# Cross-attention on one core: the right sums of the last batch's product 4 ahead of block 12, and twelve warming matmuls

## The chip, the cores and the metric

The kernel runs on one core of a Trainium2 chip. The metric is the device time of one execution in microseconds. A core has a matrix engine (TensorE, PE in the profile, with its weight loads as PEld), three engines for elementwise work (VectorE or DVE, ScalarE or ACT, GpSimd or POOL), and a queue engine that only issues transfers (SyncE or SP). The engines run their own instruction lists in order, and wait for each other through semaphores. TensorE writes into banks of an accumulator memory (PSUM), from which VectorE and ScalarE read.

## The reference

There are 8 batches of a 512 x 1024 input x1 and a context x2 of the same shape, all in f32.

```python
B, C1, C2, N = (8, 512, 512, 1024)      # D = C2 // 8 = 64
q = einsum('bcn,dc->bnd', x1, Wq) + bq
k = einsum('bcn,dc->bdn', x2, Wk) + bk[:, None]
v = einsum('bcn,dc->bdn', x2, Wv) + bv[:, None]
attn = softmax(einsum('bnd,bdm->bnm', q, k), axis=2)
out = einsum('bcm,bnm->bcn', v, attn) + x1
```

## The kernel before

Each batch goes through one call of `period`. The kernel reorders the algebra: instead of projecting values first, it multiplies the context with the exponentials of the scores (`first`, stage "y") and then the result with the value weights (`second`, stage "o"). Both are products of two 2 x 2 block matrices, done in seven block products in place of eight. These need sums and differences of blocks on the left (S1 to S4) and on the right (T1 to T4), which VectorE forms, and sums of the seven results, which VectorE forms when it empties the banks. The table `MULT` gives for each product its left and right operand, its pair of banks ("a" or "c"), and whether it opens them. In the branch that the change touches, stage "y" has the order 1, 2, 6, 5, 7, 3, 4.

Some block products are done with the same seven-fold scheme once more inside (`multiply_2`, `multiply_7`, `multiply_3`, `multiply_4`): then `inner_left` (L355) and `inner_right` (L367) form the inner sums on VectorE, `inner_product` (L374) multiplies on TensorE, two matmuls of 256 columns for each of the seven small products, and ScalarE copies some of the results out (L383). For product 4 the small products come in the order 1, 7, 6, 2, 5, 4, 3. Small product 1 takes the blocks as they are, 7 takes the third right sum, 6 the second, 5 the first and 4 the fourth. Small products 1, 6 and 5 add up in one shared bank, and ScalarE copies it after each; 7 and 4 use another, copied after 7 into a buffer v.

`multiply_3` does the matmuls of product 3 and returns a function, here called `evict_3`. When that is called, VectorE first adds v to the second half of the copies d (`complete`, L452) and then adds d to the two "a" banks to give block 12 of the y matrix (L483). Products 3 and 4 use the same buffer for v.

The right operand of product 4, called T4, is made in `sum_t4`: in the later batches ScalarE copies one block (L278), and two transfers issued by GpSimd add another on top (L280).

After products 3 and 4, `evict_y` empties the other blocks (L502) and multiplies all by the reciprocal softmax sums (L507, L505), `sum_y` forms the right sums T1 to T4 of the outer stage (L262), and `second` multiplies with the value weights in the order 1, 6, 2, 5, 7, and in the last batch 4 and 3. `evict_o` adds bias and x1 and sends the result (L526 to L539).

All of it is in an order written out by hand (`manual_schedule`): what stands first in the text is first on its engine. In batches 2 to 5 and in the last, batch 7, the branch `seven` of `period` is taken; `n` is the following batch, and None in the last one. Batches with a following one have its scores and exponentials mixed in as hooks.

The kernel begins with `head`: it issues loads of the weights, x1 and x2, clears a 128 x 128 tile named `warm` on VectorE, multiplies it with itself `WARM` times on TensorE (L635), and then projects the first batch's queries (L586) and keys (L601) as the tiles arrive. Scores (L191), the running maximum (L659, L668), the maximum over partitions on GpSimd (L221), the subtraction (L243) and the exponentials (L244) follow, up to the first large product at L321.

Of the kernel before, what the change touches and what calls it, by code (L numbers as in the profile page):

```python
# [15 lines left out]
def kernel(  # L16
# [51 lines left out]
    CT = C // P  # L68
    H = 512
    MH = N // P // 2  # L70
    WARM = 10
    lo, hi = slice(0, D), slice(D, 2 * D)

    const = ctx.enter_context(tc.tile_pool(name="const", bufs=1))
# [171 lines left out]
    def lower(s, h, i):  # L246
        e = s.e[h][:, :, i, :]
        top = s.top[h].unsqueeze(1).to_broadcast([P, 2, H])
        nc.vector.tensor_tensor(e, e, top, ALU.subtract)  # L249

    def exponential(s, h, i):
        e = s.e[h][:, :, i, :]
        nc.scalar.activation(e, e, AF.Exp)  # L253

    def exponentials(s, h, i):
        lower(s, h, i)
        exponential(s, h, i)
# [91 lines left out]
    def inner_left(s, i, x, tag):  # L349

        v = {f"{p + 1}{q + 1}": x[:, ts(q, MH // 2), ts(p, P)] for p in range(2) for q in range(2)}
        sums = sb.tile([P, 4, MH // 2, P], F32, tag=tag, name=f"aI{i}_{s.b}")
        for z, (k, x, y, op) in enumerate(LEFT):
            v[k] = sums[:, z]
            nc.vector.tensor_tensor(v[k], v[x], v[y], op)  # L355
        s.inner[i] = v

    def inner_right(s, i, x, *tags):

        v = {  # L360
            f"{q + 1}{r + 1}": x[:, ts(q, MH // 2), ts(r, H // 2)] for q in range(2) for r in range(2)
        }
        shape = [P, 4 // len(tags), MH // 2, H // 2]
        sums = [sb.tile(shape, F32, tag=t, name=f"eI{i}{t}_{s.b}") for t in tags]
        for z, (k, x, y, op) in enumerate(RIGHT):
            v[k] = sums[z // shape[1]][:, z % shape[1]]
            nc.vector.tensor_tensor(v[k], v[x], v[y], op)  # L367
        s.inner[i, "t"] = v
# [95 lines left out]
    def multiply_7(s, hooks):  # L464

        d, complete = multiply_onto(s, 7, "i2", "y12", hooks)

        def add():
            complete()
            for k in (5, 6):  # L470
                nc.vector.tensor_tensor(s.tmp[k], s.tmp[k], d, ALU.add)

        return add

    def multiply_3(s, hooks):

        d, complete = multiply_onto(s, 3, "u1", "r", hooks)

        def evict():
            complete()  # L480
            s.y["12"] = y = sb.tile([P, 2, H], F32, tag="y12", name=f"y12_{s.b}")
            for j in (1, 0):
                nc.vector.tensor_tensor(y[:, j, :], s.bank["a", j], d[:, j, :], ALU.add)  # L483

        return evict
# [4 lines left out]
    def evict_y(s, k, steps=(1, 2)):  # L490

        bank, add = RESULT[k]
        rden = s.rden.get(int(k[1]) - 1)
        if 1 in steps:
            s.y[k] = sb.tile([P, 2, H], F32, tag=f"y{k}", name=f"y{k}_{s.b}")
        y = s.y[k]
        alone = 7 in s.inner and add in (5, 6)
        for step in steps:
            for j in range(2):
                if step == 1:  # L500
                    ps, n = s.bank[bank, j], left if alone and j else slice(0, H)
                    nc.vector.tensor_tensor(y[:, j, n], ps[:, n], s.tmp[add][:, j, n], ALU.add)  # L502
                elif alone and j:
                    for x, n in ((y, left), (s.tmp[add], right)):
                        nc.vector.tensor_tensor(y[:, j, n], x[:, j, n], rden[:, n], ALU.mult)  # L505
                else:
                    nc.vector.tensor_tensor(y[:, j, :], y[:, j, :], rden, ALU.mult)  # L507
# [49 lines left out]
    def copy_first(s, h):  # L557

        s.mx[h] = sb.tile([P, 2, H], F32, tag="fold", name=f"sum_{s.b}_{h}", bufs=2)
        nc.scalar.copy(s.mx[h], s.e[h][:, :, 0, :])  # L560

    def start_sum(s, h):

        copy_first(s, h)
        for i in range(1, MH if s.b > 1 else 2):
            add_tile(s, h, i)
# [40 lines left out]
    def head(s):  # L609
# [23 lines left out]
        ps = ps_a.tile([P, H], F32, tag="a0", name="ps_warm")  # L633
        for _ in range(WARM):
            nc.tensor.matmul(ps[:, 0:P], warm, warm, start=True, stop=True)  # L635
# [72 lines left out]
    def period(s, n, nn, nnn):  # L708
# [5 lines left out]
        def first(i, hook=None):  # L714
            multiply(s, "y", i, s.a, s.t, MH, hook=hook)
# [47 lines left out]
        def add_exponential(i):  # L763
            exponential(n, 0, i)
            add_tile(n, 0, i)
# [20 lines left out]
        if seven:  # L786
            hooks = [{}, {}]
            if n:
                for i in range(MH):
                    lower(n, 0, i)  # L790
                hooks = [
                    {
                        1: lambda: copy_first(n, 0),
                        6: lambda: add_exponential(1),
                        5: lambda: add_exponential(2),
                    },
                    {6: lambda: add_exponential(3)},
                ]
            first(5, (lambda: exponential(n, 0, 0)) if n else None)
            inner_right(s, 3, s.t["22"], "eT1")  # L800
            inner_left(s, 4, s.a["22"], "a12")
            add_7 = multiply_7(s, hooks[0])
            add_7()
            evict_3 = multiply_3(s, hooks[1])
            evict_y(s, "22", (1,))
            evict_3()
            inner_right(s, 4, s.t["T4"], "eT2")
        else:
            first(5)
            if s.b == 0:  # L810
                inner_right(s, 3, s.t["22"], "eT1")
                for i in range(MH):
                    lower(n, 0, i)
            else:
                for i in range(MH):
                    exponentials(n, 0, i)
                start_sum(n, 0)
                inner_right(s, 3, s.t["22"], "eT1")
            first(7)
            if s.b > 1:  # L820
                inner_right(s, 4, s.t["T4"], "eT2")
            evict_3 = multiply_3(s, {})
            if s.b:
                evict_y(s, "22", (1,))
                evict_3()
            else:
                evict_3()
                evict_y(s, "22", (1,))
# [70 lines left out]
    with tc.manual_schedule():  # L899
        head(states[0])  # L900
        for b in range(B):
            period(*states[b : b + 4])
# [31 lines left out]
```

## Time and profile before

| | us |
|---|---|
| median of 3 runs | 693.46 (693.18 to 695.86) |
| the profiled execution | 693.62 |
| its span, first to last instruction | 691.8 |
| TensorE busy | 682.8 |
| VectorE busy | 628.9 |
| ScalarE busy | 276.1 |
| GpSimd busy | 193.5 |

A busy time is the sum of the times in which an engine had at least one instruction at work. A large f32 matmul of 128 x 512 appears as two rows, and so does each warming matmul. Rows of TensorE overlap: a new row begins before the last one has ended, so the pace is read from the starts. In a line of the timeline the first number is the start in microseconds from the beginning of the span, the second the duration, and "x8" the number of rows merged into it; brackets give the idle time of the engine just before and what ended it.

### The profile page before, as it was taken

What the parts mean: (1) busy time and instruction counts of PE and PEld (TensorE: products, weight loads), DVE (VectorE), ACT (ScalarE), POOL (GpSimd) and SP (SyncE); (2) the same over time, 40 slices, a digit from 0 to 9 for tenths busy, and PEclk for the clock granted to TensorE, in tenths of its full rate; (3) what the DMA queues carried; (4) which work ended last, traced back from release to release, by engine and by line L of the source; (5) the groups of instructions that cost most, each with busy time, mean ns of one, the idle gap of its engine ahead of it and who ended that gap; (6) DMA issues with size and microseconds to landing.
All of it is one profiled execution on the core that took longest, in us unless ns stands there. A gap on an engine that the chain in (4) does not pass through costs nothing.

```text
span 691.8 us, 6647 instructions
## 1 busy us (share of the span) xinstructions
PE 682.8 (99%) x2248; PEld 364.2 (53%) x2248; DVE 628.9 (91%) x809; ACT 276.1 (40%) x439; POOL 193.5 (28%) x147
## 2 busy tenths in 40 slices
PE   9999999999999999999999999999999999999997
PEld 5333554535545565455644566454754545545753
DVE  1999999988999889998999989999799988999785
ACT  2733353146233552345432454424544245243220
POOL 0123113522423223242142321623223232323000
PEclk9999999999999999999999999999999999999999
DMA  9676256954569754786628867198642864268303
GB/s 304 258 214 238 65 182 130 255 161 79 183 114 235 199 106 153 150 231 181 135 111 180 230 181 187 42 198 215 167 92 38 207 166 76 62 148 223 87 0 122
DMA packets 44723, 109.05 MB, mean 158 GB/s; under 512 B 4880, under 2 KB 7184, under 8 KB 44688
## 3 DMA queue, kind: packets, MB, share of 16 engines
q1 hardware_dynamic: 25856, 70.13, 30.1%
q0 software_dynamic: 17424, 36.25, 29.7%
q10 hardware_dynamic: 1408, 2.23, 1.0%
q8 instruction: 18, 0.29, 0.2%
q14 instruction: 17, 0.14, 0.1%
HBM read 72.62 MB, written 16.81 MB: 129 GB/s over the span
## 4 chain that ended last, share of the span: by engine, by line
PE 93%; DMA 3%; DVE 1%; SPq 1%; ACT 1%; issue 0%; DVEq 0%
PE ps_ya L321 24%; PE ps_i L374 17%; PE ps_oa L321 16%; PE ps_oc L321 12%; PE ps_s L191 6%; PE ps_yc L374 5%; PE ps_q L149 4%; PE ps_k L149 3%; PE ps_yc L321 3%; PE ps_ya L374 3%; DMA a<-in_x2T_dram 1%; DMA x_in_x_dram<-in_x_dram 1%; DMA x_head<-in_x_dram 1%; PE ps_sc L191 1%; PE ps_sa L191 1%; DVE aS L110 0%
## 5 line engine op out<-in xcount | busy, mean ns | idle before, releaser
L321 PE MATMUL ps_ya<-eT,aS 128*128 128x512 f32 x256 | 113.1, 595 | 0.0
L332 ACT COPY uy<-ps_ya 128x512 f32<-128x512 f32 x48 | 28.1, 588 | 139.6 <-PE ps_ya L321 126.7
L249 DVE TENSOR_TENSOR e<-e,top 128x1024 f32<-128x1024 f32 x60 | 70.5, 1228 | 11.0 <-POOL top L221 11.0
L321 PEld LDWEIGHTS ps_ya<-eT,aS 128*128 128x128 f32 x256 | 48.0, 190 | 60.9 <-issue 58.5
L253 ACT ACTIVATE e<-e 128x1024 f32<-128x1024 f32 x60 | 62.9, 1059 | 38.6 <-DVE e L249 37.1
L221 POOL PARTITION_ALL_REDUCE top<-max x16 | 32.8, 2052 | 150.8 <-DVE max L215 78.9
L226 POOL PARTITION_ALL_REDUCE den<-sum x16 | 63.4, 3961 | 40.8 <-DVE sum L215 35.8
L321 PE MATMUL ps_oa<-yT,w_S 128*128 128x512 f32 x128 | 57.6, 593 | 0.0
L321 PE MATMUL ps_oc<-y,w 128*128 128x512 f32 x128 | 57.6, 593 | 0.0
L321 PE MATMUL ps_ya<-e,a 128*128 128x512 f32 x128 | 56.3, 593 | 0.3 <-ACT e L244 0.3
L200 ACT COPY e<-ps_s 128x1024 f32<-128x1024 f32 x46 | 45.7, 1027 | 19.3 <-PE ps_s L191 17.5
L332 ACT COPY uo<-ps_oa 128x512 f32<-128x512 f32 x48 | 27.6, 584 | 54.2 <-PE ps_oa L321 44.9
L383 ACT COPY d<-ps_i 128x256 f32<-128x256 f32 x84 | 29.3, 374 | 47.7 <-PE ps_i L374 47.2
L191 PE MATMUL ps_s<-q,k 64*128 64x512 f32 x188 | 47.3, 608 | 0.8 <-ACT q L590 0.8
L551 POOL DMA_DIRECT2D uo<-in_x_dram x21 | 24.9, 1186 | 79.2 <-DVE uo L548 79.2
L555 POOL DMA_DIRECT2D sum<-e x21 | 25.7, 1222 | 66.5 <-DMA sum<-e 37.0
L321 PEld LDWEIGHTS ps_ya<-e,a 128*128 128x128 f32 x128 | 24.2, 190 | 31.3 <-issue 29.6
L321 PEld LDWEIGHTS ps_oa<-yT,w_S 128*128 128x128 f32 x128 | 24.2, 190 | 30.8 <-issue 29.9
L321 PEld LDWEIGHTS ps_oc<-y,w 128*128 128x128 f32 x128 | 24.1, 190 | 31.0 <-issue 28.9
L211 DVE TENSOR_TENSOR max<-max,e 128x1024 f32<-128x1024 f32 x30 | 36.8, 1225 | 3.0
L507 DVE TENSOR_TENSOR y<-y,den 128x512 f32<-128x512 f32 x54 | 33.8, 683 | 0.0
L238 POOL DMA_DIRECT2D den<-row x16 | 8.9, 557 | 79.0 <-DMA row<-few 73.2
(142 smaller groups left out, 1291.4 us busy)
## 6 DMA issues: line engine op xcount, KB each, us to landing
x_in_x_dram<-in_x_dram SPq DMA_DIRECT2D x60, 512.0 KB, 5.9
a<-in_x2T_dram SPq DMA_DIRECT2D x32, 512.0 KB, 7.1
sum<-e POOLq DMA_DIRECT2D x21, 512.0 KB, 5.2
uo<-in_x_dram POOLq DMA_DIRECT2D x21, 512.0 KB, 6.5
out_dram<-uo SPq DMA_DIRECT2D x21, 512.0 KB, 5.1
eT<-eT POOLq DMA_DIRECT2D x12, 512.0 KB, 6.5
den<-row POOLq DMA_DIRECT2D x16, 256.0 KB, 3.6
r<-in_x_dram POOLq DMA_DIRECT2D x7, 512.0 KB, 8.6
```

What stands on the lines that cost most here:

```text
L149: nc.tensor.matmul(ps[r, :], w_sb[:, c, :], s.x[:, c, ts(h, H)], start=(c == 0), stop=(c == CT - 1),)
L191: nc.tensor.matmul(ps[g], s.k[r, ts(i, P)], s.q[r, ts(h, H)], start=True, stop=True)
L200: nc.scalar.copy(e[:, :, i, :], whole)
L211: nc.vector.tensor_tensor(f, e[:, :, 0, :] if i == 1 else f, e[:, :, i, :], op)
L221: nc.gpsimd.partition_all_reduce(s.top[h], s.mx[h][:, 0, :], P, ReduceOp.max)
L226: nc.gpsimd.partition_all_reduce(s.den[h], s.mx[h][:, 0, :], P, ReduceOp.add)
L249: nc.vector.tensor_tensor(e, e, top, ALU.subtract)
L253: nc.scalar.activation(e, e, AF.Exp)
L321: nc.tensor.matmul(ps[:, n], left[ka][:, k, ts(j, P)], right[kb][:, k, n], start=opens and k == 0, stop=i in (2, 3, 4) and k == n_k - 1, s ...
L332: nc.scalar.copy(s.tmp[i][:, j, :], ps)
L374: nc.tensor.matmul(ps, s.inner[i][ka][:, k, :], s.inner[i, "t"][kb][:, k, :], start=opens and k == 0, stop=z in (2, 3, 4) and k == MH // 2 ...
L507: nc.vector.tensor_tensor(y[:, j, :], y[:, j, :], rden, ALU.mult)
```

## The change

In the last batch (the one with no following batch) the four right sums of product 4 are formed on VectorE before block 12 is emptied; in the other batches of the branch the order stays. The number of warming matmuls goes from ten to twelve.

```diff
-    WARM = 10
+    WARM = 12
...
             evict_3 = multiply_3(s, hooks[1])
             evict_y(s, "22", (1,))
-            evict_3()
+            if n:
+                evict_3()
             inner_right(s, 4, s.t["T4"], "eT2")
+            if not n:
+                evict_3()
```

On VectorE this gives, in the last batch, the instructions L502, L502, four times L367, L452, L483, L483, where before it was L502, L502, L452, L483, L483, four times L367. The instruction lists of ScalarE, GpSimd and SyncE are the same as before, and TensorE's differs by the two matmuls.

## The prediction

> **What bounds the kernel now.** First the shares of busy time and the slices on the page. TensorE is busy for all but 9.0 of 691.8 us, in nearly every slice, at a granted clock of 1.00 in every stretch read. So a change pays only where TensorE stands still, and costs only where it makes TensorE later.
>
> ```profile
> span 691.8 us, 6647 instructions
> PE 682.8 (99%) x2248; PEld 364.2 (53%) x2248; DVE 628.9 (91%) x809; ACT 276.1 (40%) x439; POOL 193.5 (28%) x147
> ```
>
> Next, TensorE's own list of waits (engine, line, what it waited for: us in total, times, longest). One wait stands far above the rest, and it is in the last batch: product 4 waits for VectorE's right sums (L367).
>
> ```profile
> PE ps_i L374 <- DVE eI4eT L367: 2.3, 1, 2.3
> PE ps_warm L635 <- DVE warm L632: 1.0, 1, 1.0
> PE ps_s L191 <- ACT q L590: 0.8, 1, 0.8
> ```
>
> Then the timeline around that wait (start, duration, engine, line; idle time and releaser in brackets), VectorE first. Between 653.33 and 654.49 VectorE idles for the copies of product 3; then it adds d and v, evicts block 12 (L483), and only then forms the four sums.
>
> ```profile
> 652.31 1.01 DVE L502 TENSOR_TENSOR y<-ps_yc,uy 128x512 f32<-128x512 f32 x2
> 654.49 0.69 DVE L452 TENSOR_TENSOR d<-d,v 128x512 f32<-128x512 f32 x1 [1.16 <-ACT d L383]
> 655.29 1.29 DVE L483 TENSOR_TENSOR y<-ps_ya,d 128x512 f32<-128x512 f32 x2
> 656.49 0.68 DVE L367 TENSOR_TENSOR eI4eT<-eT 128x512 f32<-128x512 f32 x1
> 657.82 0.68 DVE L367 TENSOR_TENSOR eI4eT<-eT 128x512 f32<-128x512 f32 x1
> ...
> 658.65 1.97 PE L374 MATMUL ps_i<-eI4eT,aI 128*128 128x256 f32 x8 [2.28 <-DVE eI4eT L367]
> ```
>
> Product 4 runs its small products in the order 1, 7, 6, 2, 5, 4, 3. The first needs no sum (it started at 655.34); the second needs the third sum, T3. TensorE started 0.15 us after T3 ended (657.82 + 0.68 = 658.50).
>
> Last the start. The ten warming matmuls leave twenty rows, two for each f32 matmul, and the first projection then waits for its data.
>
> ```profile
> 1.04 4.62 PE L635 MATMUL ps_warm<-warm 128*128 128x128 f32 x20 [1.04 <-DVE warm L632]
> L635 PEld LDWEIGHTS ps_warm<-warm x20: 288/333/338, 1.0 to 5.1; 128*128 128x128 f32 x20
> 5.90 1.08 PE L586 MATMUL ps_q<-x_head,wqk_sb 128*64 128x512 f32 x4 [0.23 <-DMA x_head<-in_x_dram]
> 9.35 1.96 PE L601 MATMUL ps_kc<-x_head,wqk_sb 128*64 128x256 f32 x16
> 11.50 0.65 PE L601 MATMUL ps_ka<-x_head,wqk_sb 128*64 128x256 f32 x4 [0.19 <-DMA x_head<-in_x_dram]
> ```
>
> **Part 1: the sums ahead of block 12.** Nothing is added or removed, and no DMA, matmul or copy moves: on VectorE, in the last batch alone, four 128x512 sums change places with one add and two evictions.
>
> When can the sums start? The second L502 of the pair starts at 652.91 and holds 256 columns; the next instruction follows such a one after 0.34 us (L505 to L505, 662.03 to 662.37), so at 653.25. The sums also wait for T4, which two accumulating transfers finish. They are issued by 637.05, and the longest transfer into eT takes 10.6 us to land: 647.7, 5.5 us earlier. And T4's first small product ran at 655.34 with no wait. Inside the group the starts lie 0.71, 0.61 and 0.60 apart (656.49, 657.21, 657.82, 658.42), so T3 starts at 654.57 and ends at 655.25; with the 0.15 us of release TensorE could go at 655.40.
>
> When does TensorE want it? Small products follow each other every 0.86 us (652.75, 653.61, 654.47, 655.34), so at 656.20. The slack is 0.8 us, and the wait goes entirely. Its price is best taken by pace: product 3, the same work without a stall, takes 655.34 - 649.29 = 6.05 us; product 4 takes 663.90 - 655.34 = 8.56 us. Gain **2.51 us** (the 2.28 us of visible idling and the refilling of the pipeline).
>
> What is late next? The displaced instructions:
> - The add (L452) starts after the fourth sum, at 653.25 + 1.92 + 0.60 = 655.77, and ends at 656.47 instead of 655.18. ScalarE's copy of the next v uses the same buffer; it comes 1.06 us after the second small product begins (650.16 to 651.22 in product 3), so at 657.26. Slack 0.8 us. Queued behind it on ScalarE are the copies of small products 6 and 5, and TensorE's shared bank waits for those: past this slack, each lost microsecond returns to TensorE.
> - The evictions (L483) end at 657.87. The bank is wanted by the next stage at 655.34 + 6.05 = 661.39.
> - The VectorE chain after them no longer contains the idle 1.16 us, so it runs about 1.2 us earlier, while TensorE runs 2.51 us earlier: TensorE catches up by 1.3. Tightest is the outer product 6, which needs yT2. It ends now at 663.95 + 1.22 = 665.17, afterwards at 663.97, released by 664.1; TensorE wants it at 667.33 - 2.51 = 664.82. Slack 0.7 us. Block 21 is complete at 669.19 - 1.2 = 668.0; its first half, wanted at 668.26, is ready by 667.4.
> - From there VectorE waits for TensorE (1.23 us before the next L534), and the output transfers follow it. The whole tail moves.
>
> Value taken -2.51; bounds -2.51 and, if the VectorE chain did not move up at all, 665.17 + 0.15 - 664.82 = 0.5 less, -2.0.
>
> **Part 2: two more warming matmuls.** Four more rows. The nearest row is the warming itself: its row starts lie 0.2133 us apart after the first, up to 5.26. Four more at that pace push the next free slot from 5.47 to 6.33, and the projection from 5.90 to 6.33: +0.43 us. The sixteen key rows after it have almost no pause to absorb that (eight pairs at 0.2155 are 1.72 us, and 0.05 us is lost to the DMA wait inside), so +0.37 us reaches ScalarE's key copy, and along the chain key copy, scores, maximum, all-reduce, subtraction, exponential, everything up to the first large product at 24.96. VectorE goes through that stretch back to back, so nothing there takes it up. The exponential that waits for the last warming matmul (L645, 5.70) may slip by 0.86 us freely: ScalarE's next work is at 9.59.
>
> [...] The projection already runs at full pace from 5.90 (two rows per 0.43 us). [...] By the row, +0.37. [...]
>
> [...]
>
> **Sum.** -2.51 + 0.2 = -2.3 us. On the profiled execution: span 691.8 to 689.5, its time 693.62 to 691.3. The median of the runs, 693.46, stands 0.16 lower: **691.2 us**, -0.33%. What a measurement of this kernel can tell from no change is about 0.5% or 3.5 us, which is more than the entire wait.
>
> **Rivals.**
> - *The wait moves instead of going.* If the VectorE chain stays where it is, outer product 6 waits 0.5 us: 691.7. For: the margin is only 0.7 us. Against: 1.16 us of VectorE idling really is filled.
> - *It does not do what it says.* If the last arrival was T4's transfer and not T3, nothing is won: 693.46 + 0.2 = 693.7. Against: T4's raw block was multiplied at 655.34 without waiting.
> [...]
> - *Slower.* The head's delay makes the next batch's context load collide. That load is issued from 36.78 on, after the queries, and TensorE's keys wait for its last tile at 46.88. If a 2 MB block of another queue went ahead of it at the 404 GB/s of the head, 5.2 us: 691.2 + 5.2 = 696.4. It decides once the load lands 2.3 us later than now, the whole gain. For: TensorE waits there already. Against: a shift of 0.2 us moves issue and need alike.
>
> **How the numbers follow.** The forecast 0.80 (its own range 690.6 to 691.8: head 0 to +0.37, product 4 -2.51 to -2.3, and some tenths between runs), wait moved 0.07, no effect 0.04, faster 0.05, slower 0.04. The range of 690.2 to 692.8 takes in the moved wait and the scatter of the three runs (a median may lie some tenths off; one run was 2.4 us above it), and leaves out the last three cases. Faster than 690.0 (over 0.5%): the late-release case and a little, 0.06. Slower than 696.9: the far end of the collision, 0.03. Within: 0.91.
>
> **What would show it.** Right: TensorE's wait on L367 is gone, product 4 takes 6.05 us like product 3, and VectorE shows the four L367 between L502 and L452 with little or no idling ahead of L452. The first projection starts between 5.9 and 6.35 and the first large product at 24.96 to 25.35. Wrong: a wait of TensorE on L262 or on ScalarE's copies (L383) after 656; a projection later than 6.4; a wait of the keys at 46.9 that has grown by more than some tenths; or a longer span with none of these.

## The result, and the profile after

The changed kernel took 691.11 us in the median (690.91 to 691.7, six runs), the kernel before 693.54 (693.17 to 695.86, six runs). The ratio is 0.995 with a 95% interval of 0.9931 to 0.9968. The time and the span of the profiled execution (691.33 and 689.5 us) are those forecast. The forecast of "within 0.5%" is not borne out: the interval excludes no change, and 0.5% is in its middle, although the medians differ by 0.35% only. The means (694.12 and 691.20 us) differ by 0.42%, since two of the six runs of before stand at 695.44 and 695.86. Where such runs come from is the main finding below.

First the page of the changed kernel and its list of TensorE's waits, complete (engine, line, what it waited for: us in total, times, longest):

```profile
span 689.5 us, 6656 instructions
PE 683.1 (99%) x2252; PEld 365.3 (53%) x2252; DVE 630.4 (91%) x809; ACT 275.7 (40%) x439; POOL 189.3 (27%) x147
```

```profile
PE ps_warm L635 <- DVE warm L632: 1.0, 1, 1.0
PE ps_s L191 <- ACT q L590: 0.8, 1, 0.8
PE ps_ya L321 <- ACT e L244: 0.3, 1, 0.3
PE ps_i L374 <- ACT e L200: 0.3, 1, 0.3
PE ps_q L586 <- DMA x_head<-in_x_dram: 0.2, 1, 0.2
```

TensorE's idle time fell from 691.8 - 682.8 = 9.0 us to 6.4 us, and the wait of 2.3 us for L367 is no longer in the list. The timeline at the same place, VectorE and then TensorE (start, duration):

```profile
652.55 1.01 DVE L502 TENSOR_TENSOR y<-ps_yc,uy 128x512 f32<-128x512 f32 x2
653.48 0.68 DVE L367 TENSOR_TENSOR eI4eT<-eT 128x512 f32<-128x512 f32 x1
...
654.80 0.68 DVE L367 TENSOR_TENSOR eI4eT<-eT 128x512 f32<-128x512 f32 x1
655.40 0.68 DVE L367 TENSOR_TENSOR eI4eT<-eT,eI4eT 128x512 f32<-128x512 f32 x1
656.01 0.68 DVE L452 TENSOR_TENSOR d<-d,v 128x512 f32<-128x512 f32 x1
656.79 1.29 DVE L483 TENSOR_TENSOR y<-ps_ya,d 128x512 f32<-128x512 f32 x2
...
655.57 1.03 PE L374 MATMUL ps_i<-eT,a 128*128 128x256 f32 x4
656.43 1.89 PE L374 MATMUL ps_i<-eI4eT,aI 128*128 128x256 f32 x8
...
661.61 3.60 PE L321 MATMUL ps_oa<-y,w 128*128 128x512 f32 x8
```

The third sum ends at 655.48; TensorE takes it at 656.43, with no pause after the first small product. Product 4 takes 661.61 - 655.57 = 6.04 us, where it took 8.56. VectorE has no idle time ahead of L452 any more.

At the start of the span:

```profile
1.04 5.38 PE L635 MATMUL ps_warm<-warm 128*128 128x128 f32 x24 [1.04 <-DVE warm L632]
6.63 3.65 PE L586 MATMUL ps_q<-x_head,wqk_sb 128*64 128x512 f32 x16 [0.20 <-DMA x_head<-in_x_dram]
...
25.44 1.12 PE L321 MATMUL ps_ya<-e,a 128*128 128x512 f32 x2 [0.30 <-ACT e L244]
...
44.22 3.96 PE L149 MATMUL ps_k<-x_in_x_dram,wqk_sb 128*64 128x512 f32 x16
48.11 0.70 PE L321 MATMUL ps_ya<-eT,aS 128*128 128x512 f32 x1
```

The last product of these stood here in the kernel before:

```profile
47.88 0.70 PE L321 MATMUL ps_ya<-eT,aS 128*128 128x512 f32 x1
```

The projection starts 0.73 us later than in the profile before (5.90). Warming ended at 6.42, and by the trace's record the last transfer that the projection waits for landed at 6.49, against 5.76 before. So the data came last in this execution, but only 0.07 us behind the warming. The first large product is 0.48 us late (25.44 for 24.96): a part is gone already at the first keys, whose last rows waited for data at 11.50 before and start at 11.89 now. At the keys of the next batch, where TensorE waits for data anyway, half of the rest is gone: the product after them is 0.23 us late. Sum: -2.52 + 0.23 = -2.29 us; the spans differ by 2.3.

### The profile page after: what moved, and what is told of

Read it like the earlier page. It is cut to its first block, busy times and chain, and to the rows that moved or that the text cites. A ratio compares the mean times of both kernels' runs of the same rounds, so it can differ in the third digit from the quotient of the medians.

```text
span 689.5 us, 6656 instructions
## 1 busy us (share of the span) xinstructions
PE 683.1 (99%) x2252; PEld 365.3 (53%) x2252; DVE 630.4 (91%) x809; ACT 275.7 (40%) x439; POOL 189.3 (27%) x147
## 4 chain that ended last, share of the span: by engine, by line
PE 94%; DMA 3%; SPq 1%; ACT 1%; DVE 1%; issue 0%; DVEq 0%
PE ps_ya L321 24%; PE ps_i L374 17%; PE ps_oa L321 16%; PE ps_oc L321 12%; PE ps_s L191 6%; PE ps_yc L374 5%; PE ps_q L149 4%; PE ps_k L149 3%; PE ps_ya L374 3%; PE ps_yc L321 3%; DMA a<-in_x2T_dram 1%; DMA x_in_x_dram<-in_x_dram 1%; DMA x_head<-in_x_dram 1%; PE ps_sc L191 1%; PE ps_sa L191 1%; DVE aS L110 0%
## 5 line engine op out<-in xcount | busy, mean ns | idle before, releaser
L226 POOL PARTITION_ALL_REDUCE den<-sum x16 | 59.2, 3701 | 40.8 <-DVE sum L215 35.8
L548 DVE SCALAR_TENSOR_TENSOR uo<-ps_oc,bv_sb,uo 128x512 f32<-128x512 f32 x42 | 29.5, 741 | 1.6 <-PE ps_oc L321 1.6
```

The costliest lines, as they stand in the source:

```text
L226: nc.gpsimd.partition_all_reduce(s.den[h], s.mx[h][:, 0, :], P, ReduceOp.add)
```

## The experiments

All runs of the kernel before that stood beside these experiments are counted together: 60 runs in three sets. They fall into two groups by the mean clock that the trace shows as granted to TensorE. Thirty-three runs have 0.999 or 1.000 and a median of 693.47 us; twenty-seven (8 of 23, 14 of 22 and 5 of 15) have 0.997 or 0.998 and a median of 695.15. Two runs do not fit: one at 695.38 with a full clock, and one at 697.73 in the second group; nothing here explains them. The question behind most of the runs is where the second group comes from.

**The sums alone**

```diff
-    WARM = 12
+    WARM = 10
```

(against the changed kernel)

> The sums moved, ten warming matmuls as before. Theory A (the sums alone bring 2.5 us, and the two warming matmuls cost next to nothing because the first projection waits for its data at about 6 us anyway): most runs 690.7 to 691.2 us, and product 4 takes 6.05 us. Theory B (ten warming matmuls leave some executions in which the matrix engine stays longer at half pace, twelve do not): beside those, some runs some 2.2 us higher, near 693, as two of six runs of the kernel before stood 2.2 us above the others. Without B, all runs within 0.8 us.

Measured: 691.25 us (690.52 to 691.83, five runs), ratio to before 0.9955 (0.9942 to 0.9969), all at a clock of 0.999 or 1.000. Within the scatter the sums alone are the whole gain. Theory B expected some runs near 693 with ten warming matmuls; none of the five is there.

**The warming alone**

```diff
-    WARM = 10
+    WARM = 12
```

(against the kernel before)

> The sums stay where they were, twelve warming matmuls. Theory A: 693.2 to 693.7 us, the median of before within 0.3 us, TensorE still waits 2.3 us for the sums of product 4. Theory B: no run near 695.6, so all within 0.8 us, while the kernel before keeps its two levels. If the warming cost its full row pace: 693.9.

Measured: 693.49 us (692.91 to 695.73, twelve runs), ratio 0.9995 (0.9981 to 1.0009). Theory B falls: four of the twelve runs stand at 695.27 to 695.73, with twelve warming matmuls. The median is as theory A had it. One of the four is the profiled one, and its windows show what theory B had looked for in the wrong place (length, busy time and rows of TensorE, granted clock, share and GB/s of the transfers), with the timeline's lines of the same stretch below:

```profile
656.40:659.05 2.65, 0.37 (x2) 1.00 0.01 3
659.05:662.50 3.45, 3.45 (x8) 0.51 0.00 0
662.50:664.30 1.80, 1.80 (x10) 1.00 0.00 0
```

```profile
655.74 1.03 PE L374 MATMUL ps_i<-eT,a 128*128 128x256 f32 x4
659.05 3.65 PE L374 MATMUL ps_i<-eI4eT,aI 128*128 128x256 f32 x8 [2.28 <-DVE eI4eT L367]
662.54 1.03 PE L374 MATMUL ps_yc<-eT,a 128*128 128x256 f32 x4
```

Behind the stall TensorE runs at half clock: eight rows take 3.49 us from the first start to the next group's (659.05 to 662.54). The kernel before needed 1.80 in its profiled execution, from 658.65 to the line below:

```profile
660.45 1.03 PE L374 MATMUL ps_yc<-eT,a 128*128 128x256 f32 x4
```

The difference is 1.7 us, the distance between the two groups (695.15 - 693.47 = 1.68). No profile of the kernel before in its second group was kept: that these runs lose their time at this place is concluded from here and from the runs that follow. This gave theory C: the stall that the change removes costs twice, once as waiting and, in some executions, once more as a lower clock after it.

**Fewer and more warming matmuls, with the sums moved**

```diff
-    WARM = 12
+    WARM = 6
```

> The sums moved, six warming matmuls. They end at about 3.9 us, so TensorE has a gap of some 2 us before the projection's data. Theory A alone (warming is only a filler): the same 691.1 us, as the projection starts with its data at 5.9 to 6.6. Theory B (the gap keeps the clock at half pace): the projection's rows lie 0.85 us apart per pair in place of 0.43, up to some 3.4 us longer, and most runs stand 1.5 to 2.5 us higher, at 692.5 to 693.5.

Measured: 692.9 us (691.13 to 693.68, eleven runs), ratio 0.9979 (0.9969 to 0.9989): 1.65 us above the kernel with ten. In the profile the projection started with its data, but at half pace:

```profile
1.04 2.93 PE L635 MATMUL ps_warm<-warm 128*128 128x128 f32 x12 [1.04 <-DVE warm L632]
6.29 6.37 PE L586 MATMUL ps_q<-x_head,wqk_sb 128*64 128x512 f32 x16 [2.31 <-DMA x_head<-in_x_dram]
L586 PE MATMUL ps_q<-x_head,wqk_sb x16: 593/1057/1113, 6.3 to 12.1; 128*64 128x512 f32 x16
```

Sixteen rows took 6.37 us in place of 3.65 (the third line, of the view by source line, gives the shortest, median and longest row in ns; the median was 592 with twelve). The warming rows had run at the pace of those with twelve (their median is 421 ns in both), and full pace shows only at the end of the queries (the shortest row) and in the sixteen key rows from 12.48 on, which took 1.91 us, with twelve 1.93. So in this execution, with a gap of 2.3 us ahead of the projection, the full pace came later, and warming up to about the data's arrival was worth some 1.7 us here. Too few warming matmuls cost time; more than ten do not:

```diff
-    WARM = 12
+    WARM = 16
```

> The sums moved, sixteen warming matmuls. Theory A with its other half (warming past the arrival of the data delays the projection): warming ends at 7.1 to 7.9 us, the projection starts 0.5 to 1.3 us later than with twelve, of which the wait for the keys' data at 45 to 47 us absorbs about 0.3: 691.4 to 692.1. Theory B: all runs on one level. If warming is free: 691.1.

Measured: 691.22 us (690.81 to 691.62, five runs), ratio 0.9957 (0.9945 to 0.9968). The projection started at 6.84 in the profile, straight behind the warming, 0.2 us after that with twelve, and nothing of it reaches the time beyond the scatter. The later start of 0.5 to 1.3 us that was expected is refuted for this execution: its warming ended at 6.90, since the later rows ran at full pace (32 rows in 5.86 us, 24 in 5.38).

**Half of the move**

```diff
             evict_3 = multiply_3(s, hooks[1])
             evict_y(s, "22", (1,))
-            evict_3()
+            if n:
+                evict_3()
+            else:
+                evict_3.first()
             inner_right(s, 4, s.t["T4"], "eT2")
+            if not n:
+                evict_3(False)
```

(the main cut; `first` is the add of v, `evict_3(False)` the two evictions without it; against the kernel before)

> Ten warming matmuls; only the two evictions of block 12 go behind the sums, the add of v stays ahead of them. The third sum should end at 657.1 us and TensorE lose 1.06 us in place of 2.45. [...] Median 693.45 - 1.4 = 692.1 us. Theory D (the higher level comes from elsewhere): a third of the runs at 693.9.

Measured: 691.96 us (691.65 to 692.27, five runs), ratio 0.9957 (0.9944 to 0.9969), all at a clock of 1.000. The wait shrank to 0.9 us:

```profile
PE ps_i L374 <- DVE eI4eT L367: 0.9, 1, 0.9
```

0.14 us from the expectation, and no run of the higher group, as theory C has it if 0.9 us of idling is too short; theory D expected a third of the runs at 693.9.

**A longer stall**

```diff
-            for j in (1, 0):
+            for j in (1, 0) * (1 if s.b < B - 1 else 2):
```

(in the eviction of block 12; against the kernel before)

> Ten warming matmuls, the sums where they were before, the two evictions of block 12 done twice in the last batch (the same values again): the stall grows by 1.2 us to some 3.5 us. [...] Theory D: one third of the runs high as before, median 694.7.

Measured: 696.18 us (694.72 to 697.53, ten runs), ratio 1.0019 (1.0007 to 1.003). Two runs at 694.72 and 694.85 with a clock of 0.999, eight at 695.83 to 697.53 with 0.998 or less. The wait was 3.5 us:

```profile
PE ps_i L374 <- DVE eI4eT L367: 3.5, 1, 3.5
```

Eight of ten in the higher group, where theory D expected one of three.

```diff
-            for j in (1, 0):
+            for j in (1, 0) * (1 if s.b < B - 1 else 3):
```

> As the longer stall, with the two evictions done three times: a stall of some 4.7 us. Theory C: every run has the half clock after the stall, so all at 695.9 + 1.7 = 697.6 us. Theory D: one third high, median 695.9.

Measured: 698.18 us (697.66 to 701.12, six runs), ratio 1.0052 (1.0035 to 1.0068). All six have a clock of 0.997 or less; the wait and the windows after it:

```profile
PE ps_i L374 <- DVE eI4eT L367: 4.7, 1, 4.7
```

```profile
656.70:661.40 4.70, 0.12 (x1) 1.00 0.00 2
661.50:665.30 3.80, 3.80 (x10) 0.55 0.00 0
665.40:668.00 2.60, 2.60 (x13) 1.00 0.00 0
```

The median is 0.6 above theory C's, and one run at 701.12 is explained by nothing here. Five of the six have a mean clock of 0.995, where the profiled one has 0.997; its 3.80 us at 0.55 amount to an estimated 3.4 us at half clock, or 0.25% of the span, so the five seem to have had two such stretches. No profile of such a run was kept, and what the second costs stays open. Theory D, with 695.9, is out.

**The stall filled**

```diff
             inner_product(s, i, z, *steps[z])
+            if z == 1 and i == 4 and s.b == B - 1:
+                warm = states[0].warm
+                for _ in range(8):
+                    nc.tensor.matmul(s.both[:, 1, 0:P], warm, warm, start=True, stop=True)
             if z in hooks:
```

(the main cut; against the kernel before. `s.both` is the bank tile whose first half receives small product 7, and its second half is unused, so nothing reads what is written there. The kernel's description above lets small product 4 share this tile; in the code of product 4 it goes straight into a "c" bank.)

> Ten warming matmuls, the order of before, the wait for the sums stays; eight 128x128 matmuls of the warming tile into an unused half bank stand in TensorE's list between small products 1 and 7 of the last product 4, some 1.75 us at full pace inside the 2.45 us of the stall. Theory C (idling, not waiting, costs the clock): all runs at 693.4 us, none near 695.3, although the wait is as long as before. Theory D: one third of the runs 1.8 us higher, as before.

Measured: 693.73 us (693.2 to 696.23, eleven runs), ratio 0.9989 (0.9977 to 1.0). No run has a clock below 0.999. TensorE still starts on the third sum as late as before (658.74 for 658.65), but idles for 0.41 us only:

```profile
656.38 1.95 PE L451 MATMUL ps_i<-warm 128*128 128x128 f32 x16
658.74 1.99 PE L374 MATMUL ps_i<-eI4eT,aI 128*128 128x256 f32 x8 [0.41 <-DVE eI4eT L367]
```

With 27 of 60 runs of before and none of eleven here, it is the idling and not the lateness that costs the clock. The one run at 696.23 had a full clock and stays unexplained.

**The changed kernel again**

No edit; the changed kernel beside the kernel before.

> The changed kernel itself once more, beside the kernel before on the same chip, to count the runs with half clock after the stall. Theory C: the kernel before has them in a third to two thirds of its runs, at about 695.2 us and a mean granted clock of 0.998 or less, the others at 693.4; the changed kernel has none, all runs 690.8 to 691.8 us, clock 0.999 or 1.000. Theory D: the changed kernel shows the higher level too, at about 693.

Measured: 690.69 us (690.55 to 691.21, five runs) against 693.7 (693.04 to 695.33, fifteen runs), ratio 0.9953 (0.994 to 0.9967). Five of the fifteen runs of before have a clock of 0.997, and stand at 694.72 to 695.33; no run of the changed kernel has one below 0.999. Over all runs with the sums fully moved and ten or more warming matmuls that makes none of 21.

**The sums first in the other batches too**

```diff
-            if n:
-                evict_3()
             inner_right(s, 4, s.t["T4"], "eT2")
-            if not n:
-                evict_3()
+            evict_3()
```

> The changed kernel, with the sums of product 4 ahead of block 12 in batches 2 to 5 as well. There TensorE does the next batch's scores between products 3 and 4 and has no wait for the sums, so nothing can be won; the third scores want the first 'a' bank 1.8 us after product 3 ends, at 252.2 us in the first of these batches, and block 12 would leave it at about 252.9 in place of 251.5. A wait of some 0.8 us in each of four batches: 691.1 + 3.1 = 694.2 us. If a move past work that nobody waits for were free: 691.1.

Measured: 694.04 us (693.47 to 694.46, eleven runs), ratio to before 1.0 (0.9991 to 1.0009): the whole gain is given back. The wait stands where it was expected, four times:

```profile
PE ps_sa L191 <- DVE y L483: 2.0, 4, 0.5
```

```profile
250.76 1.99 PE L191 MATMUL ps_s<-q,k 64*128 64x512 f32 x8
253.24 1.13 PE L191 MATMUL ps_sa<-q,k 64*128 64x512 f32 x4 [0.49 <-DVE y L483]
```

In the changed kernel the next outer product of that batch starts at 263.94, here at 264.89, after a start of the scores that differs by 0.19: 0.76 us in the batch, 3.0 in four.

## Why the prediction was right and wrong

*Part 1, product 4.* Right for executions at full clock, in every term that was worked out. T3 was forecast to end 0.8 us ahead of TensorE and did so (655.48 for 656.43, a margin of 0.95 less the release); product 4 took 6.04 us for a forecast of 6.05; the tail moved as a whole, and TensorE met no wait of its own in it. The rivals of a moved wait and of no effect are out by the list of waits, and so is the collision at the next batch's keys: TensorE's wait of 0.23 us there (46.88 in the profile before) is no longer in the list.

*The step of the mechanism that failed: "Value taken -2.51".* It counted the stall as lost waiting only, with "granted clock of 1.00 in every stretch read", which was one execution. In 27 of 60 executions of the kernel before, the mean clock is lower and the time 1.7 us longer, which the runs put down to half clock behind the same stall. On the means that term is 694.35 (all 60 runs) - 693.59 (the 33 at full clock) = 0.76 us. Without it the gain is 693.59 - 691.12 (the 21 runs of the changed order) = 2.47 us, with it 3.23 us or 0.47%. That the -0.33% of the forecast meets the medians is in part luck: the median of the first three runs of before lay in the lower group; in one set, where fourteen of 22 runs were in the higher one, the median of before was 695.1.

*The step behind "within": "What a measurement of this kernel can tell from no change is about 0.5% or 3.5 us, which is more than the entire wait".* It gave the 0.91 for "within", and it failed even without the missing term. The intervals of the experiments reach 0.1 to 0.2% to either side, and the lowest of the 33 runs of before at full clock (693.03) lies above the highest of the 21 (691.83), so a gain of 0.35% is told from none. The three times of before, 693.18, 693.46 and 695.86, were read as scatter; with their distance of 2.4 us they look like the two groups, though the clock of the third is not on record.

*Part 2, the +0.2 us of the sum.* No run shows this term, which was the author's estimate, and the times neither confirm nor refute it: ten, twelve and sixteen warming matmuls with the sums moved give 691.25, 691.11 and 691.22; twelve without them has a ratio of 0.9995 (0.9981 to 1.0009). Two of the prediction's own signs spoke against it: the projection began later than 6.4 (6.63), and the first large product later than 25.35 (25.44). What the runs showed in its place is that the push of the projection to 6.33 depends on the execution. In the profile of twelve warming matmuls alone, the twenty-four rows took 5.49 us and the projection started behind them at 6.46 without a wait for data; in the profile after, they took 5.38 us and the data set the start, with a wait of 0.20 us. Twenty rows took 4.62 us in the profile before and 3.92 in that of the sums alone, where the projection then waited 1.14 us for its data and started at 6.11. That data can come later than in the profile before, as in the profile after, was left out of this term. And the late start was in part absorbed, at the first keys and at the keys of the next batch, which the prediction had passed through almost in full.

*The clock.* At the head six warming matmuls lost some 1.7 us, and more than ten brought nothing. The clock should have been weighed at the stall in product 4 too, where the runs with a lower one are none of five at 0.9 us of idling, 27 of 60 at 2.3, eight of ten at 3.5, six of six at 4.7.

*The late-release case*, which the chances name, was a loss of clock at the projection that more warming cures. No run with ten warming matmuls or more shows its gain: with ten and the sums moved no run stands on a higher level, and with twelve alone four of twelve do, of which the profiled one lost the clock behind the stall.

## What to carry to other kernels

Price a stall of the matrix engine by its length and by what the clock does after it: here 2.3 us of idling cost 2.5 us always and 1.7 us more in nearly half of the executions, which one profile at full clock cannot show. A stall that cannot be removed can be filled: matmuls whose result nobody reads kept the clock here. When the runs of a kernel stand on two levels, put the mean granted clock of each run beside its time before calling it scatter. An order that frees one engine early is worth it only in the batch where that engine is waited for; in the others the work that it displaces was on time, and then was not.

## What the runs showed of the hardware

The half clock behind a stall ended after about 3.4 us in each of the three profiled executions that had it. With twelve warming matmuls alone the granted clock is 0.77, 0.50 and 0.87 in the stretches of 2 us from 658, 660 and 662; in the longer stall 0.57 in those from 660 and from 662; in the longest 0.55 in the 3.80 us from 661.50. An estimate from these shares, with half clock where the full one is missing: 3.4 us each time. Behind these stretches it reads 1.00 again.

The length of a stall alone did not decide it. The kernel before and the kernel with twelve warming matmuls alone have the same stall of 2.28 us in their profiles. In the first the clock reads 1.00 behind it (658.60 to 662.10), in the second 0.51 (659.05 to 662.50). What decides it in one execution is not shown.

At the start the warming rows of 128 columns lie 0.2133 us apart in the profile before, where eight rows of 256 columns in product 3 take 1.72 us (650.16 to 651.88), 0.215 us each; so they run at half pace. A weight load of 128 columns took 0.333 us there and 0.190 in product 4. How long this lasts varied: the sixteen query rows behind the warming ran at full pace in the profile after (3.65 us), at half pace for most of their time in the one with six warming matmuls (6.37 us). The granted clock does not tell: in the latter profile the stretch in which most query rows took 1.06 us shows 1.00.

```profile
6.20:11.80 5.60, 5.51 (x14) 1.00 1.06 338
```

Around the stalls the column agreed with the pace of the rows in the stretches shown here (0.51 where eight rows took 3.49 us in place of 1.80); at the start the duration of a known row is the better clock.
